# LoRA products of a gated FFN as six-row products in four row groups of TensorE, with another PSUM layout and another place for the fold transpositions

## The chip, the cores and the metric

The kernel runs on one NeuronCore of a Trainium2 chip (trn2). Its metric is the device time in microseconds, as a median over runs. Five engines work side by side: PE (TensorE, matrix products), DVE (VectorE), ACT (ScalarE), POOL (GpSimd) and SP (SyncE, which here only issues transfers). PE reads from SBUF and writes to PSUM, which has eight banks of 512 fp32 values for each of 128 partitions.

## The reference

One post-norm transformer block over 2 x 1024 tokens of width 1024, in fp32. The first half is a gated unit of hidden width 2752 in which, for each token, the half of the silu values of the smallest magnitude is set to zero. The second half is a gated FFN with quantised-style weights (a quarter of the input width, repeated four times) and LoRA terms of rank 2. Cut to what matters here:

```python
def _qlora_linear(x, wq, A, B):
    w = jnp.tile(wq, (1, 4))
    base = x @ w.T
    lora = x @ A.T @ B.T
    return base + lora * 0.5

def _L0_ffn_ref(x, w1q, a1, b1, w3q, a3, b3, w2q, a2, b2):   # h = 2752, d = 1024, rank 2
    gate = silu(_qlora_linear(x, w1q, a1, b1))
    up = _qlora_linear(x, w3q, a3, b3)
    return _qlora_linear(gate * up, w2q, a2, b2)

x = layernorm(x + attn(x, w_gate, w_up, w_down))
x = layernorm(x + ffn(x, w1q, a1, b1, w3q, a3, b3, w2q, a2, b2))
```

## The kernel before

The 2048 tokens are 16 tiles of 128, in four groups of four tiles (`GT = 4`). The program runs through three parts: `gate_up` (products with w_gate and w_up, and the search for the median magnitudes), `down` (products with w_down, then the first layernorm), and the FFN. Every fp32 product is made of products of a rounded high part and a low part (fp32r): high by high, high by low, low by high. `split` makes the two parts, the high one on ACT (L173), the low one on POOL or DVE (L174).

The FFN works group by group (`ffn`). It has two halves:

- **f1**, the first products. Since the weights repeat four times along the input, the token's 1024 values are first added up to 256 ("fold", on POOL, L927 to L929), so that a product has two chunks of 128. The hidden width 2752 is cut into eight column blocks of 344 (`NB`, `BW`). An item is one tile and one block: `f1_mm` makes gate and up products in two PSUM banks (a pair), ACT takes silu of the first (L987), DVE multiplies it by the second (L988) and by the two rows of a2 (L990), ACT sums those (L992), POOL adds the results of blocks that share second weights into hf (L994). The order is block by block, and in a block tile by tile.
- **f2**, the second products. hf is transposed (L1026), split into hh and hl (L1028, L1029), and multiplied by w2 in `run_ops` (L765); cm holds the last 48 columns and the LoRA sums. Then come the residual sum (L768) and the layernorm.

The LoRA term of f1 is x A^T B^T. The four numbers x A^T of each token (two for gate, two for up) are in `dall`. `f1_tile` writes them into a tile tl, for each of gate and up six columns: high part, high part again, low part. `f1_tile2` transposes the two fold chunks (L949) and two shifted views of tl (L951), so that each of gate and up has its six rows at the top of its own 128-row matrix in fh; ACT copies (L954), DVE makes the low part fl (L955). The tile br holds, in rows 0 to 5 and 32 to 37, the B weights of gate and up in the matching order (high, low, high), with zeros elsewhere. A LoRA product is then one ordinary product of 128 rows, last in its bank (L984):

```python
for c in range(2):
    nc.tensor.matmul(o, fh[:, c, :], wh[:, c, :], start=c == 0, stop=False)      # L981
    nc.tensor.matmul(o, fh[:, c, :], wl[:, c, :], start=False, stop=False)       # L982
    nc.tensor.matmul(o, fl[:, c, :], wh[:, c, :], start=False, stop=False)       # L983
nc.tensor.matmul(o, fh[:, 2 + w, :], self.br[:, bs], start=False, stop=True)     # L984
```

So an item has 14 products of 128 x 128 by 128 x 344, and two of them are LoRA products: 16 tiles x 8 blocks x 2 = 256 in all.

br is built during the last `down` group by `ffn_consts`: SP loads the raw rows (L810), ACT and POOL split them, and two small copies on ACT's own transfer queue (L813) put the low part in place. The four tiles of the first group are prepared in that time too (`f1_first`); those of the following groups while the group before them is in f1.

What sets the order: `item` keeps two queues. It calls an item's loads at once, its preparation up to two items later and its products up to two more items later (`q1`, `q2`), so that loads are issued ahead and `down` runs into the FFN without a stop; `flush` empties both queues. A scheduler then orders the recorded instructions for each engine; on the chip each engine runs its own list in order, and waits on semaphores for the others. PSUM from `down` on is one pool, psb: three pairs of banks, tag mm, for products, and two single banks, tag tp, for transpositions. A buffer is handed on in rotation, when its last reader is done.

Of the kernel before, what the change touches and what calls it, by code (L numbers as in the profile page):

```python
# [7 lines left out]
F = mybir.dt.float32  # L8
# [10 lines left out]
P = 128  # L19
# [46 lines left out]
class Kern:  # L66
# [8 lines left out]
    def run(self):  # L75
# [3 lines left out]
        with ExitStack() as es:  # L79
# [38 lines left out]
            self.gate_up()  # L118
            self.lasta = self.lastv = self.lastd = None
            ps_es.close()  # L120
            psb = es.enter_context(tc.tile_pool(name="psb", bufs=1, space=PSUM, reuse_waits="tile"))
            self.pair = lambda: psb.tile([P, 2, 512], F, tag="mm", bufs=3, name="mm")
            self.tpb = lambda: psb.tile([P, 4, P], F, tag="tp", bufs=2, name="tp")
            x_es.close()
# [18 lines left out]
            self.fcg = self.ffn_consts()  # L143
            list(self.down(ng - 1, f1=2))
            self.dp_es, self.fp2 = dp_es, None
            for g in range(ng):
                self.ffn(g)
            self.flush()
# [640 lines left out]
    def ffn_consts(self):  # L789
        nc, fp = self.nc, self.fp  # L790
        A = self.A
        self.br = fp.tile([P, NI], R, name="br")
        self.abc = fp.tile([P, 4, H], F, name="abc")
        self.fst, self.c2 = {}, False
        for i in range(4):
            yield
            with self.load_behind():
                nc.sync.dma_start(
                    self.abc[:, i, :], A[("a1", "a3")[i // 2]][i % 2 : i % 2 + 1, :].partition_broadcast(P)
                )  # L800
        for b in range(NB):
            yield
            bs = slice(b * BW, (b + 1) * BW)
            sv = fp.tile([P, 2, BW], F, tag="sv", bufs=2, name="braw")
            raw, lo = sv[:, 0], sv[:, 1].bitcast(R)
            nc.gpsimd.memset(raw, 0.0)
            with self.load_behind():
                for w, n in ((0, "b1t"), (32, "b3t")):
                    for i in range(3):
                        nc.sync.dma_start(raw[w + 2 * i : w + 2 * i + 2, :], A[n][:, bs])  # L810
            self.split(self.br[:, bs], lo, raw)
            for w in (0, 32):
                nc.scalar.dma_start(self.br[w + 2 : w + 4, bs].bitcast(F), lo[w + 2 : w + 4, :].bitcast(F))  # L813

    def dots_down(self):
        xt, a1, a3 = (self.tk.tile([P, NI], F, tag=f"a{i}", name=n) for i, n in ((0, "dx"), (1, "da"), (3, "db")))
# [37 lines left out]
    def ffn(self, g):  # L854
        tiles = [t for t in range(g * GT, (g + 1) * GT) if t < self.nt]
        for b in range(NB):
            ws = []
            if tiles[-1] + 1 < self.nt:
                if b % 2 == 0:
                    if b:  # L860
                        self.f1_tile2(tiles[-1] + b // 2)
                    self.f1_tile(tiles[-1] + 1 + b // 2)
            for t in tiles:
                self.item(
                    lambda: self.f1_prep(b, ws),
                    lambda: None,
                    lambda st=self.fst[t], b=b, ws=ws: self.f1_mm(st, b, ws),
                    2, 2,
                )
        if tiles[-1] + 1 < self.nt:  # L870
            self.f1_tile2(tiles[-1] + GT)
        ws = []
        for t in tiles:
            self.item(
                lambda: self.f2_w(ws),
                lambda t=t: self.f2_prep(self.fst[t], t),
                lambda st=self.fst[t], t=t, ws=ws: self.f2_mm(st, t, ws),
                2, 1,
            )

# [34 lines left out]
    def f1_tile(self, t, f=None):  # L915
# [13 lines left out]
        G.tensor_tensor(f, f, x2[:, 768:1024], ALU.add)  # L929
        dr = sm.tile([P, 4], R, tag="dr", name="dr")  # L930
        V.tensor_copy(dr, d)
        tl = fp.tile([P, P + 6], F, tag="tl", bufs=1, name="tl")
        G.memset(tl, 0.0)
        d2 = d.rearrange("p (w r) -> p w r", w=2)
        dr2 = dr.bitcast(F).rearrange("p (w r) -> p w r", w=2)
        for w in range(2):
            q = 38 * w
            V.tensor_copy(tl[:, q : q + 2], dr2[:, w])
            V.tensor_copy(tl[:, q + 2 : q + 4], dr2[:, w])
            V.tensor_tensor(tl[:, q + 4 : q + 6], d2[:, w], dr2[:, w], ALU.subtract)  # L940
        st["f"] = f, tl

    def f1_tile2(self, t):
# [3 lines left out]
        tp = self.tpb()  # L947
        for c in range(2):
            nc.tensor.transpose(tp[:, c, :], f[:, c * P : (c + 1) * P], self.ident)  # L949
        for w in range(2):  # L950
            nc.tensor.transpose(tp[:, 2 + w, :], tl[:, 6 * w : 6 * w + P], self.ident)  # L951
        fh = fp.tile([P, 4, P], R, tag="fh", bufs=6, name="fh")
        fl = fp.tile([P, 2, P], R, tag="fl", bufs=6, name="fl")
        nc.scalar.copy(fh, tp)  # L954
        V.tensor_tensor(fl, tp[:, 0:2, :], fh[:, 0:2, :].bitcast(F), ALU.subtract)  # L955
        st["f"] = fh, fl

    def f1_mm(self, st, b, ws):
        nc, fp = self.nc, self.fp
        V, G = nc.vector, nc.gpsimd  # L960
        bs = slice(b * BW, (b + 1) * BW)
# [10 lines left out]
            st["hf"] = self.fp2.tile([P, 688], F, tag="hf", bufs=5, name="hf")  # L972
            st["part"] = self.sm.tile([P, 2, NB], F, tag="part", bufs=6, name="part")
        hf, part = st["hf"], st["part"]
        pp = self.pair()
        ps = [pp[:, w, :BW] for w in range(2)]
        for w in range(2):
            o = ps[w]
            wh, wl = ws[w]
            for c in range(2):  # L980
                nc.tensor.matmul(o, fh[:, c, :], wh[:, c, :], start=c == 0, stop=False)  # L981
                nc.tensor.matmul(o, fh[:, c, :], wl[:, c, :], start=False, stop=False)  # L982
                nc.tensor.matmul(o, fl[:, c, :], wh[:, c, :], start=False, stop=False)  # L983
            nc.tensor.matmul(o, fh[:, 2 + w, :], self.br[:, bs], start=False, stop=True)  # L984
        hs = slice((b % 2) * BW, (b % 2 + 1) * BW)
        gt = hf[:, hs] if b < 2 else self.fp2.tile([P, BW], F, tag="gt", bufs=3, name="gt")
        nc.scalar.activation(gt, ps[0], AF.Silu)  # L987
# [104 lines left out]
```

## Time and profile before

| | us |
|---|---|
| median of 3 runs | 1923.64 |
| lowest and highest | 1919.69, 1924.59 |
| the profiled execution, its own time | 1926.91 |
| its span, first to last instruction | 1925.1 |
| first f1 product in it | 1466.5 |

The profile is of one execution; its granted TensorE clock was 0.993 of full speed. Its page gives busy times and shares of the span for each engine, groups of instructions by line with their mean duration, and what ended the idle time ahead of them. L984 is line 984 of the kernel above. A product's recorded duration contains the time in which it drains, and the next one may start before it ends; so durations of PE rows can't be added up, and start-to-start distances are used instead. PEld rows are the weight loads, one for each product. ACTq, SPq and the like are instructions of an engine's sequencer, such as the issue of a transfer. In the table by stage the cuts are where f1 begins and ends in each group.

### The profile page before, as it was taken

How to read it: one execution, taken by the hardware profiler on the slowest of the kernel's cores; microseconds unless marked ns; L12 is line 12 of the kernel's file. 1: busy time of each engine (PE TensorE's matmuls, PEld its weight loads, DVE VectorE, ACT ScalarE, POOL GpSimd, SP SyncE). 2: the span in 40 equal slices, each digit the busy share in tenths (PEclk: the TensorE clock that was granted, in tenths of full speed). 3: DMA queues.
4: the chain of work that ended last, by engine and by line, in shares of the span. 5: the costliest groups of instructions: out<-in, count | busy, mean ns of one | idle time of the engine just before them, and what ended most of it. 6: DMA issues, size and time to landing. Idle time of an engine off the chain costs nothing. (4 is left out here: it accounts for less than half of the span.)

```text
span 1925.1 us, 29381 instructions
## 1 busy us (share of the span) xinstructions
PE 1885.3 (98%) x10825; PEld 1754.4 (91%) x10825; DVE 1229.6 (64%) x1831; ACT 904.0 (47%) x1448; POOL 973.0 (51%) x606
## 2 busy tenths in 40 slices
PE   9999999999999999999999999999998999998998
PEld 9999999999999999999888787888787979898896
DVE  4633556767358574691238998688467857779565
ACT  4333477414883258622246533323333746557362
POOL 5655664445445354355565443554565746436062
PEclk9999999999999999999999999999999999999999
DMA  7677687676977868667798756977776878485651
GB/s 266 237 250 260 236 325 261 210 272 253 330 231 241 314 235 303 236 228 256 282 328 285 270 188 227 337 245 261 268 250 244 279 284 321 155 318 177 229 196 66
DMA packets 166205, 488.66 MB, mean 254 GB/s; under 512 B 24772, under 2 KB 45380, under 8 KB 166056
## 3 DMA queue, kind: packets, MB, share of 16 engines
q1 hardware_dynamic: 165848, 486.43, 71.9%
q8 instruction: 85, 1.39, 0.3%
q14 instruction: 64, 0.52, 0.1%
q10 hardware_dynamic: 208, 0.31, 0.0%
HBM read 370.30 MB, written 116.33 MB: 253 GB/s over the span
## 5 line engine op out<-in xcount | busy, mean ns | idle before, releaser
L174 POOL TENSOR_TENSOR wl<-wr,wh 128x1376 fp32r<-128x1376 f32 (+2 forms) x187 | 566.4, 3035 | 466.1 <-ACT wh L173 436.8
L353 PE MATMUL mm<-wh,xh 128*128 128x344 f32 x1928 | 610.4, 322 | 2.8 <-DMA wh<-tw3T1h 2.8
L353 PE MATMUL mm<-wh,xl 128*128 128x344 f32 x1928 | 609.8, 320 | 0.0
L173 ACT CAST wh<-wr 128x1376 fp32r<-128x1376 f32 (+2 forms) x192 | 232.4, 1215 | 340.9 <-PE mm L353 199.6
L353 PEld LDWEIGHTS mm<-wh,xh 128*128 128x128 f32 x1928 | 364.7, 189 | 3.0 <-issue 3.0
L353 PEld LDWEIGHTS mm<-wh,xl 128*128 128x128 f32 x1928 | 364.6, 189 | 0.0
L353 PE MATMUL mm<-wl,xh 128*128 128x344 f32 x1928 | 342.1, 319 | 0.0
L353 PEld LDWEIGHTS mm<-wl,xh 128*128 128x128 f32 x1928 | 310.1, 188 | 0.0
L765 PE MATMUL mm<-wh,mh 128*128 128x512 f32 x680 | 217.8, 400 | 0.1
L765 PE MATMUL mm<-wl,mh 128*128 128x512 f32 x680 | 215.1, 395 | 1.1 <-POOL wl L174 1.1
L765 PE MATMUL mm<-wh,ml 128*128 128x512 f32 x648 | 205.5, 396 | 0.8 <-DVE ml L750 0.8
L460 ACT ACTIVATE jk<-a,cur 128x2752 int8<-128x2752 f32 x66 | 170.8, 2588 | 31.2 <-DVE cur L482 15.8
L994 POOL TENSOR_TENSOR hf<-hf,gt 128x344 f32<-128x344 f32 x96 | 142.2, 1491 | 75.6 <-DVE gt L988 68.7
L725 POOL TENSOR_TENSOR m<-m,ub 128x512 f32<-128x512 f32 (+2 forms) x93 | 111.0, 1194 | 128.0 <-ACT ub L724 65.8
L981 PE MATMUL mm<-wh,fh 128*128 128x344 f32 x512 | 166.2, 325 | 5.8 <-DVE gt L988 5.2
L983 PE MATMUL mm<-wh,fl 128*128 128x344 f32 x512 | 164.0, 320 | 0.0
L982 PE MATMUL mm<-wl,fh 128*128 128x344 f32 x512 | 163.9, 320 | 0.0
L765 PEld LDWEIGHTS mm<-wl,mh 128*128 128x128 f32 x680 | 127.4, 188 | 30.1 <-POOL wl L174 2.2
L768 DVE TENSOR_TENSOR acc<-acc,mm 128x1024 f32<-128x1024 f32 x96 | 116.4, 1214 | 57.9 <-PE mm L765 27.8
L765 PEld LDWEIGHTS mm<-wh,mh 128*128 128x128 f32 x680 | 124.7, 189 | 24.8 <-ACT mh L749 0.5
L765 PEld LDWEIGHTS mm<-wh,ml 128*128 128x128 f32 x648 | 121.2, 189 | 26.9 <-DVE ml L750 1.0
L992 ACT ACTIVATE pa<-pa 128x344 f32<-128x344 f32 x256 | 123.0, 483 | 38.6 <-DVE pa L990 34.0
(191 smaller groups left out, 2742.5 us busy)
## 6 DMA issues: line engine op xcount, KB each, us to landing
wr<-wu SPq DMA_DIRECT2D x64, 688.0 KB
wr<-wg SPq DMA_DIRECT2D x52, 688.0 KB
wr<-wd SPq DMA_DIRECT2D x48, 512.0 KB
s_d<-cc SPq DMA_DIRECT2D x64, 344.0 KB
m_d<-mt SPq DMA_DIRECT2D x64, 344.0 KB
a<-s_d SPq DMA_DIRECT2D x64, 344.0 KB
wl<-wc_w SPq DMA_DIRECT2D x48, 344.0 KB
wh<-wc_w SPq DMA_DIRECT2D x48, 344.0 KB
```

What stands on the lines that cost most here:

```text
L173: self.lasta = self.nc.scalar.copy(hi, raw)
L174: (eng or self.nc.gpsimd).tensor_tensor(lo, raw, hi.bitcast(F), ALU.subtract)
L353: self.nc.tensor.matmul(o, l, r, start=start and n < m and n % (2 * KH) == 0, stop=stop and n >= m and (n - m) % KH == KH - 1)
L460: nc.scalar.activation(jk.bitcast(I8), av[j], AF.Sign, bias=t, scale=-1.0, accum_out=s)
L725: nc.gpsimd.tensor_tensor(m[:, :w], m[:, :w], ub[:, :w], ALU.mult)
L765: nc.tensor.matmul(ps[:, h], a, b[:, h * 512 : (h + 1) * 512], start=i == 0, stop=i == len(ops) - 1)
L768: nc.vector.tensor_tensor(out, out, ps.rearrange("p a b -> p (a b)"), ALU.add)
L981: nc.tensor.matmul(o, fh[:, c, :], wh[:, c, :], start=c == 0, stop=False)
L982: nc.tensor.matmul(o, fh[:, c, :], wl[:, c, :], start=False, stop=False)
L983: nc.tensor.matmul(o, fl[:, c, :], wh[:, c, :], start=False, stop=False)
L992: nc.scalar.activation(pa[:, r], pa[:, r], AF.Copy, scale=0.5, accum_out=part[:, r, b : b + 1])
L994: G.tensor_tensor(hf[:, hs], hf[:, hs], gt, ALU.add)
```

## The change

- **LoRA products.** tl gets 128 columns. The six columns of gate and up stand at 0 and 32 for even tiles and at 64 and 96 for odd tiles; one transposition instead of two brings them to the same rows of fh, which now has three chunks. br's rows 0 to 63 are copied to rows 64 to 127, by one more transfer for each block on ACT's queue. For every second tile, `f1_mm` takes two PSUM pairs at once and opens all four banks with four products of six rows each, at rows 0, 32, 64 and 96, which are four row groups of the array; they stand first in their banks. The 12 other products of each tile follow.
- **PSUM.** After the last `down` group both queues are flushed and psb is closed. A new pool psc gives the FFN four pairs; a transposition takes a pair too, and uses its first bank.
- **Fold transpositions.** `f1_tile` and `f1_tile2` for the next group's tiles were called while an item's loads were recorded. Now they are called with the item's products, two to four items later, ahead of the first product of the block.

```diff
@@ run
-            psb = es.enter_context(tc.tile_pool(name="psb", bufs=1, space=PSUM, reuse_waits="tile"))
+            psb_es = ExitStack()
+            psb = psb_es.enter_context(tc.tile_pool(name="psb", bufs=1, space=PSUM, reuse_waits="tile"))
...
             self.dp_es, self.fp2 = dp_es, None
+            self.flush()
+            psb_es.close()
+            psc = es.enter_context(tc.tile_pool(name="psc", bufs=1, space=PSUM, reuse_waits="tile"))
+            self.pair = lambda: psc.tile([P, 2, 512], F, tag="mm", bufs=4, name="mm")
+            self.tpb = lambda: self.pair()[:, 0].rearrange("p (a b) -> p a b", a=4)
@@ ffn_consts
+            nc.scalar.dma_start(self.br[64:P, bs].bitcast(F), self.br[0:64, bs].bitcast(F))
@@ ffn
-            if tiles[-1] + 1 < self.nt:
-                if b % 2 == 0:
-                    if b:
-                        self.f1_tile2(tiles[-1] + b // 2)
-                    self.f1_tile(tiles[-1] + 1 + b // 2)
+            pre = []
+            if tiles[-1] + 1 < self.nt and b % 2 == 0:
+                if b:
+                    pre.append(lambda b=b: self.f1_tile2(tiles[-1] + b // 2))
+                pre.append(lambda b=b: self.f1_tile(tiles[-1] + 1 + b // 2))
...
-                    lambda st=self.fst[t], b=b, ws=ws: self.f1_mm(st, b, ws),
+                    lambda st=self.fst[t], t=t, b=b, ws=ws, pre=pre: ([pre.pop(0)() for _ in pre[:]], self.f1_mm(st, t, b, ws)),
@@ f1_tile
-        tl = fp.tile([P, P + 6], F, tag="tl", bufs=1, name="tl")
+        tl = fp.tile([P, P], F, tag="tl", bufs=1, name="tl")
...
-            q = 38 * w
+            q = 32 * w + t % 2 * 64
@@ f1_tile2
-        for w in range(2):
-            nc.tensor.transpose(tp[:, 2 + w, :], tl[:, 6 * w : 6 * w + P], self.ident)
-        fh = fp.tile([P, 4, P], R, tag="fh", bufs=6, name="fh")
+        nc.tensor.transpose(tp[:, 2, :], tl, self.ident)
+        fh = fp.tile([P, 3, P], R, tag="fh", bufs=6, name="fh")
...
-        nc.scalar.copy(fh, tp)
+        nc.scalar.copy(fh, tp[:, 0:3])
@@ f1_mm
-        pp = self.pair()
-        ps = [pp[:, w, :BW] for w in range(2)]
+        if t % 2 == 0:
+            self.pp = [self.pair() for _ in range(2)]
+            for j in range(2):
+                for w in range(2):
+                    q = slice(64 * j + 32 * w, 64 * j + 32 * w + 6)
+                    nc.tensor.matmul(
+                        self.pp[j][:, w, :BW], self.fst[t + j]["f"][0][q, 2, :], self.br[q, bs], start=True, stop=False
+                    )
+        ps = [self.pp[t % 2][:, w, :BW] for w in range(2)]
...
-                nc.tensor.matmul(o, fh[:, c, :], wh[:, c, :], start=c == 0, stop=False)
+                nc.tensor.matmul(o, fh[:, c, :], wh[:, c, :], start=False, stop=False)
                 nc.tensor.matmul(o, fh[:, c, :], wl[:, c, :], start=False, stop=False)
-                nc.tensor.matmul(o, fl[:, c, :], wh[:, c, :], start=False, stop=False)
-            nc.tensor.matmul(o, fh[:, 2 + w, :], self.br[:, bs], start=False, stop=True)
+                nc.tensor.matmul(o, fl[:, c, :], wh[:, c, :], start=False, stop=c == 1)
```

More of the change, by code (lines that the diff above doesn't have):

```diff
@@ L866, in ffn @@
                     lambda: None,
-                    lambda st=self.fst[t], b=b, ws=ws: self.f1_mm(st, b, ws),
+                    lambda st=self.fst[t], t=t, b=b, ws=ws, pre=pre: ([pre.pop(0)() for _ in pre[:]], self.f1_mm(st, t, b, ws)),
                     2, 2,
                 )
-        if tiles[-1] + 1 < self.nt:
-            self.f1_tile2(tiles[-1] + GT)
+        pre = [lambda: self.f1_tile2(tiles[-1] + GT)] if tiles[-1] + 1 < self.nt else []
         ws = []
@@ L876, in ffn @@
                 lambda t=t: self.f2_prep(self.fst[t], t),
-                lambda st=self.fst[t], t=t, ws=ws: self.f2_mm(st, t, ws),
+                lambda st=self.fst[t], t=t, ws=ws, pre=pre: ([pre.pop(0)() for _ in pre[:]], self.f2_mm(st, t, ws)),
                 2, 1,
@@ L949, in f1_tile2, with f1_mm @@
             nc.tensor.transpose(tp[:, c, :], f[:, c * P : (c + 1) * P], self.ident)
-        for w in range(2):
-            nc.tensor.transpose(tp[:, 2 + w, :], tl[:, 6 * w : 6 * w + P], self.ident)
-        fh = fp.tile([P, 4, P], R, tag="fh", bufs=6, name="fh")
+        nc.tensor.transpose(tp[:, 2, :], tl, self.ident)
+        fh = fp.tile([P, 3, P], R, tag="fh", bufs=6, name="fh")
         fl = fp.tile([P, 2, P], R, tag="fl", bufs=6, name="fl")
-        nc.scalar.copy(fh, tp)
+        nc.scalar.copy(fh, tp[:, 0:3])
         V.tensor_tensor(fl, tp[:, 0:2, :], fh[:, 0:2, :].bitcast(F), ALU.subtract)
         st["f"] = fh, fl
-    def f1_mm(self, st, b, ws):
+    def f1_mm(self, st, t, b, ws):
         nc, fp = self.nc, self.fp
```

## The prediction

> **What bounds the kernel now.** I read the page's totals and its 40 slices first, then the table by stage, then the PE rows in order of time inside two stages, and the list of waits last.
>
> ```profile
> span 1925.1 us, 29381 instructions
> ...
> PE 1885.3 (98%) x10825; PEld 1754.4 (91%) x10825; DVE 1229.6 (64%) x1831; ACT 904.0 (47%) x1448; POOL 973.0 (51%) x606
> ```
>
> Of these, only PE is near the span. The change touches the FFN, the last 460 us, so the stages there count. In the table by stage below, the columns are PE, PEld, DVE, ACT and POOL busy (instructions), granted clock, DMA share and GB/s. The four rows are the four first-FFN stages (f1), one for each group of four token tiles.
>
> ```profile
> 1466.50:1551.40 84.90, 80.30 (x483) 76.76 (x482) 70.33 (x117) 56.96 (x168) 60.64 (x49) 0.98 0.81 278
> ...
> 1589.20:1662.40 73.20, 73.20 (x470) 72.92 (x469) 53.63 (x104) 47.44 (x157) 47.64 (x43) 1.00 0.77 277
> ...
> 1696.90:1775.10 78.20, 74.57 (x471) 72.95 (x470) 72.01 (x109) 59.08 (x179) 42.73 (x37) 1.00 0.73 245
> ...
> 1810.60:1882.40 71.80, 71.80 (x458) 71.59 (x457) 46.87 (x76) 45.55 (x155) 37.51 (x26) 1.00 0.66 229
> ```
>
> In the second and fourth stages PE never rests; every other engine has 20 us or more to spare. In the third, DVE is busy 72.0 of 78.2 us, and PE waits for it. The PE rows in order of time give the price of one product (start, duration):
>
> ```profile
> 1818.86 0.32 PE L983 MATMUL mm<-wh,fl 128*128 128x344 f32 x1
> 1819.02 0.32 PE L984 MATMUL mm<-br,fh 128*128 128x344 f32 x1
> 1819.17 0.32 PE L981 MATMUL mm<-wh,fh 128*128 128x344 f32 x1
> ```
>
> Starts lie 0.157 us apart although a product takes 0.32 us: a product costs 0.157 as long as the next may enter while it drains. L984 is the LoRA product, at the full price although only 6 of its 128 rows carry data. What a product costs when nothing may overlap shows where PE had run dry:
>
> ```profile
> 1754.52 0.32 PE L984 MATMUL mm<-br,fh 128*128 128x344 f32 x1
> 1755.41 0.42 PE L981 MATMUL mm<-wh,fh 128*128 128x344 f32 x1 [0.57 <-DVE gt L988]
> 1755.67 0.32 PE L982 MATMUL mm<-wl,fh 128*128 128x344 f32 x1
> ```
>
> The first product after the gap is 0.42 long and the second starts 0.26 behind it: 0.105 us more than in the stream, for a weight load that nothing covered. So draining costs 0.32 - 0.157 = 0.163 and restarting 0.105.
>
> **The change part by part.** The order in which the changed program's instructions stand tells what the scheduler made of it, and I work from that.
>
> *Removed:* 256 products L984: 256 x 0.157 = -40.2 us. One of two transpositions of tl per tile: 16 at the 0.11 us by which transpositions follow each other: -1.8.
>
> *Added products:* 256 six-row products. In the source four stand together, for two tiles. In the compiled order only 21 fours are left; 86 groups are pairs, since the second tile's two products were put later, behind their wait for a free PSUM pair. That is 107 groups instead of 64. If the members of a group run beside each other, a group costs one product: 107 x 0.157 = +16.8. No row of this trace has less than 128 rows, so it can't say whether they do. The nearest row, the transpositions' 0.11 us for each 128-column weight load, would add 149 further members x 0.11 = +16.4. The Trainium skill (TensorE: Matmul & The Clock Gate, Part 3: Packing small matmuls) has products in different row groups start about 4 ns apart, +0.6. The transpositions all use the same rows and are not near in just that, so I take the page's and keep +16.4 for the range.
>
> *Added switches of the array:* each group goes from 128-row to 32-row products and back, 214 switches. This is where a rule speaks against the change. The trace shows only one form, 128 by 128, always overlapped. The Trainium skill (TensorEngine Tiling (Array Packing), Key Properties) says that changing the tiling mode, unlike changing the tile, drains the engine. By the rows alone, without the rule, the switches are free and the sum is -30 us. With it, each switch lets the product in flight run out (0.163), and the next weight load is uncovered (0.105, the restart above): 0.268 x 214 = +57.4. The bounds for one switch are 0 and 0.352 (0.163 plus a whole recorded weight load of 0.189). I take 0.268, the trace's own price for running dry and restarting.
>
> *Fold transpositions later:* at the opening of the first stage, PE's order has three tiles' transpositions at its head, with f1 work behind them:
>
> ```profile
> 1478.78 0.41 PE L951 MATMUL tp<-ident,tl 128*128 128x128 f32 x2 [0.38 <-DVE tl L940]
> 1481.06 0.44 PE L949 MATMUL tp<-ident,fold 128*128 128x128 f32 x2 [1.87 <-POOL fold L929]
> 1481.34 0.38 PE L951 MATMUL tp<-ident,tl 128*128 128x128 f32 x2
> 1482.23 0.42 PE L981 MATMUL mm<-wh,fh 128*128 128x344 f32 x1 [0.51 <-DVE hf L988]
> ```
>
> Four gaps between 1477.5 and 1482.2 hold 3.6 us beyond the work, and the clock then stands at 0.50 from 1483.2 to 1486.6, worth 1.7. In the new order these transpositions stand eight items (a tile and a column block each) apart. Bounds -5.3 and 0; I take -4. In the new order the first h transpositions of the closing FFN half (f2) also stand two items before the end of f1; before, PE waited there for ACT's copy hh, with gaps of 3.0, 0.9 and 1.0 us in stages one to three. I take -3 of 4.9. POOL's memset of tl becomes 128 columns (3.4 us in all before), and ACT's fh copy three quarters as long (9.3 us in all, under PE): nothing, covered by 10 us or more of POOL and ACT idle time per stage.
>
> *Four PSUM pairs, two taken at a time:* the third stage's five waits PE mm L981 <- DVE gt L988 (4.8 us of gaps between its PE rows) are PE being ahead of DVE. With 29 groups costing PE 29 x (0.157 + 0.536) = 20.1 us in place of 64 x 0.157 = 10.0, PE falls behind DVE, and these waits go: -4. Against it, a transposition now takes one of the four pairs, so a pair returns one tile earlier than before. What stands behind such a wait on PE is the rest of the stage; the scheduler moved the second tile's products behind up to 11 others to cover it. Some 12 times, 0.25 us, bounds 0 and 1 each: +3.
>
> *Flush, br and the queues:* flush finishes the down products before the FFN loads; SP's first w1 load now stands behind four 512 KB weight loads and the last masks. Eight new 88 KB copies of br stand on ACT's queue. Each waits until two earlier copies have landed, and with it ACT and everything behind, above all mh, which PE needs. How that looks is in the trace:
>
> ```profile
> 1366.88 5.28 ACTq L813 DMA_DIRECT2D br<-braw  x3
> 1372.26 0.59 ACT L749 CAST mh<-tp 128x512 fp32r<-128x512 f32 x1 [6.39 <-DMA br<-braw]
> ```
>
> A stop of 6.4 us; PE, with three items queued, lost 1.8 us soon after it. Eight more issues at 0.57 us and their waits lie mostly under that cover. If it is gone each costs PE one or two us. Together +3, bounds -1 and +12.
>
> *Sum:* -40.2 - 1.8 - 4 - 3 - 4 + 16.8 + 57.4 + 3 + 3 = +27.2 us. The profiled execution took 1926.91 (span 1925.1), so 1954; against the median of 1923.64 that is 1951.
>
> **The rivals.** *The switch is free and the groups overlap* (faster). The sum without 57.4 is -30.2. But then DVE stays ahead in time in the third stage: PE needs 384 x 0.157 + 29 x 0.157 + 1.3 = 66 us, DVE 72, so that stage ends at 74 at the earliest, not at 68; +5.7. That gives -24.5: 1899. For it: rows with gaps show PE restarting at once, and the weight loads run ahead of products in flight. Against: the rule. The deciding point is one switch at 0.141 us ((57.4 - 27.2) / 214): below it the kernel is faster, above it slower.
>
> *Only the tail is paid,* 0.163 a switch, weights loaded meanwhile: -22.5 on my sum, 1928. For it: weight loads lie 0.157 ahead of their products everywhere in the stream. Against: a load for another mode may itself have to wait.
>
> *Dear switches and paced groups:* 0.352 a switch (+18) and members 0.11 apart (+16.4): 1985. For it: the weight loads' busy share, 91%, leaves this lane little room.
>
> *It doesn't do what it says* holds in part already: 86 of 107 groups are pairs. Were all 64 fours kept, 43 x 0.693 = 30 us less would be paid and my sum would be about -3; so the split is what makes the likeliest case slow.
>
> **How the numbers follow.** A measurement of this kernel can tell about 0.3% (6 us) from no change. My case 0.38 (1940 to 1965), tail only 0.20 (1918 to 1940), dear 0.20 (1965 to 2000), free 0.22 (1890 to 1912). Faster: the free case and a fringe of the tail case, 0.25. Same: the middle of the tail case, 0.07. Slower: 0.68. The range cuts half of the free case and half of the dear one: 1898 to 1983.
>
> **What would show it.** In the stream of f1, the gap from the last 128-row start to a group's first start, and from its last start to the next 128-row start: 0.43 each in my case (0.157 + 0.268), 0.32 for the tail, 0.16 if free. Between members: near zero, or 0.11. Stages two and four: with 27 and 23 groups at 0.693 in place of 64 products at 0.157 each, 73.2 and 71.8 us should become some 81 and 78; in the free case 67 and 65. The opening of the first stage should show no gap over 1 us. If PE has gaps of over 1 us before the groups with DVE as releaser, the pair waits were underestimated; if the down stage before 1466 grows by more than 5 us, br's copies were.

## The result, and the profile after

The changed kernel takes 1942.43 us (median of 6 runs, 1940.50 to 1948.87) against 1921.51 for the kernel before (6 runs): +20.9 us, ratio 1.0111 with a 95% interval of 1.0096 to 1.0125. It is slower, inside the range, 9 us below the predicted 1951. The sum behind that number is right only in total: two of its terms are wrong, in opposite directions.

The profiled execution took 1943.85 us. The page's totals:

```profile
span 1942.1 us, 29330 instructions
...
PE 1903.1 (98%) x10809; PEld 1734.8 (89%) x10809; DVE 1243.3 (64%) x1831; ACT 903.1 (46%) x1448; POOL 977.4 (50%) x606
```

PE's busy time grew by 17.8 us and the span by 17.0. The table by stage, with the columns as before (length, then PE, PEld, DVE, ACT, POOL busy, granted clock, DMA share, GB/s):

```profile
1467.90:1556.40 88.50, 81.74 (x464) 70.45 (x464) 75.64 (x108) 59.18 (x175) 62.22 (x48) 0.94 0.80 277
1592.80:1670.00 77.20, 76.85 (x463) 66.63 (x463) 57.12 (x107) 47.46 (x158) 44.41 (x39) 1.00 0.75 265
1705.90:1790.10 84.20, 80.76 (x463) 68.86 (x463) 74.23 (x113) 59.01 (x181) 48.05 (x38) 0.96 0.65 224
1825.70:1900.10 74.40, 73.67 (x455) 64.99 (x455) 50.25 (x77) 44.87 (x154) 36.10 (x26) 1.00 0.62 223
```

Stages two and four, where PE had no rest before, went from 73.2 and 71.8 us to 77.2 and 74.4. I had said 81 and 78, or 67 and 65 with free switches: it is between. Stages one and three also lost clock, 0.94 and 0.96 for 0.98 and 1.00.

The rows of PE in order of time (start, duration) show a group of four among full products:

```profile
1829.80 0.32 PE L995 MATMUL mm<-wh,fl 128*128 128x344 f32 x1
1830.05 0.43 PE L985 MATMUL mm<-br,fh 6*128 6x344 f32 x4
1830.41 0.42 PE L993 MATMUL mm<-wh,fh 128*128 128x344 f32 x1
1830.67 0.31 PE L994 MATMUL mm<-wl,fh 128*128 128x344 f32 x1
1830.83 0.32 PE L995 MATMUL mm<-wh,fl 128*128 128x344 f32 x1
```

L985 is the six-row product, L993 to L995 are the full ones. As medians over the whole trace: 0.250 from the last full start to the group's first start, 0.003 from one member to the next, 0.350 from the last member to the next full start, 0.262 from that to the second one, 0.157 from there on. Four six-row products run as one, as I had taken them to. A group costs 0.250 + 0.350 + 0.262 - 2 x 0.157 = 0.55 us, 0.549 with the unrounded medians (pairs add one 0.003 and fours three). Of that 0.157 is the product itself, so the two switches cost 0.392. The weight loads of the same stretch (PEld) show what the price is made of:

```profile
1829.64 0.19 PEld L995 LDWEIGHTS mm<-wh,fl 128*128 128x128 f32 x1
1830.05 0.19 PEld L985 LDWEIGHTS mm<-br,fh 6*128 6x128 f32 x4 [0.22 <-issue]
1830.41 0.19 PEld L993 LDWEIGHTS mm<-wh,fh 128*128 128x128 f32 x1 [0.17 <-issue]
1830.52 0.19 PEld L994 LDWEIGHTS mm<-wl,fh 128*128 128x128 f32 x1
```

In the stream a load starts 0.154 us ahead of its own product, beside the product in flight: L995 at 1829.64 for the product at 1829.80. At a switch it does not. The loads of the group, and later that of the first full product, start together with their own product (0.002 ahead in the median), and that product's row is 0.42 long instead of 0.32. So each switch, in either direction, costs a wait until the load may start and then a load that nothing covers. Going in, the wait is 0.250 - 0.157 = 0.093; its uncovered load, 0.105, lies inside the group's row. Coming out, the wait is 0.350 - 0.105 - 0.157 = 0.088; its load shows as 0.262 instead of 0.157 ahead of the second full product. That is some 0.2 us for each switch, where I had 0.268: 0.163 of wait and 0.105 of load.

The opening of the first stage, with its 3.6 us of gaps before, is now one dense stream; transpositions stand between items, and PE waits for none of them:

```profile
1485.98 0.32 PE L995 MATMUL mm<-wh,fl 128*128 128x344 f32 x1
1486.14 0.38 PE L955 MATMUL mm<-ident,fold 128*128 128x128 f32 x2
1486.36 0.27 PE L956 MATMUL mm<-ident,tl 128*128 128x128 f32 x1
1486.56 0.42 PE L985 MATMUL mm<-br,fh 6*128 6x344 f32 x2
```

But the same stage has a larger gap 48 us later (the bracket holds PE's idle time and its releaser):

```profile
1534.19 0.32 PE L995 MATMUL mm<-wh,fl 128*128 128x344 f32 x1
1539.39 0.65 PE L985 MATMUL mm<-br,fh 6*128 6x344 f32 x2 [4.88 <-DVE gt L999]
1539.97 0.66 PE L993 MATMUL mm<-wh,fh 128*128 128x344 f32 x1
```

The group waits for a free PSUM pair, and that pair for DVE's product gt (L999). DVE's and POOL's rows of the same stretch say why gt was late:

```profile
1534.17 1.58 DVE L180 TENSOR_TENSOR wl<-wr,wh 128x688 fp32r<-128x688 f32 x1
1535.67 2.30 DVE L946 TENSOR_TENSOR tl<-dall,dr 128x2 f32<-128x2 f32 x1
...
1538.83 0.93 DVE L999 TENSOR_TENSOR gt<-gt,mm 128x344 f32<-128x344 f32 x2
```

```profile
1534.98 2.97 POOL L180 TENSOR_TENSOR wl<-wr,wh 128x1024 fp32r<-128x1024 f32 x1
```

A weight split and the next tile's tl stand ahead of gt in DVE's list. L946 subtracts two columns, 0.15 us as a rule, and here takes 2.30: it ends with POOL's split, at 1537.97 and 1537.95. It is not the whole of the gap: ACT's two silus for gt (L998) ran from 1535.70 to 1536.48, so by an estimate from these rows the first pair could have been free near 1536.6, and about 2 of the 4.9 us would have remained. The third stage has a gap of its own, where the h transpositions (L1037), now inside f1, wait for POOL; the row by stretch below it gives the granted clock, the value after the POOL column:

```profile
1779.13 0.44 PE L1037 MATMUL mm<-ident,hf 128*128 128x128 f32 x2
1782.27 0.90 PE L1037 MATMUL mm<-ident,hf 128*128 128x128 f32 x3 [2.71 <-POOL hf L1005]
```

```profile
1783.10:1788.00 4.90, 4.90 (x17) 3.94 (x16) 2.42 (x8) 2.93 (x11) 1.90 (x2) 0.50 0.11 35
1539.40:1549.60 10.20, 10.20 (x34) 8.57 (x35) 8.43 (x11) 6.66 (x22) 5.93 (x5) 0.51 0.96 347
```

Behind each of the two gaps PE runs at half clock, for 6.8 and 10.2 us.

On ACT's queue the new copies (L820) stand where I had them; the stop of 6.4 us is as long as before, and the first f1 product comes at 1467.9 instead of 1466.5:

```profile
1364.96 5.01 ACTq L819 DMA_DIRECT2D br<-braw  x3
1370.07 0.59 ACT L755 CAST mh<-tp 128x512 fp32r<-128x512 f32 x1 [6.40 <-DMA br<-braw]
...
1373.96 1.18 ACTq L820 DMA_DIRECT2D br<-br  x2
```

**An account of the four f1 stages.** I compared each start-to-start distance on PE with the usual one of its kind (0.157 between full products, the distances above at groups, 0.11 and 0.246 at transpositions). What is left over is put down to waits, or to half clock (a granted clock of 0.5) where the clock was low; the usual distances are medians, and a wait can end inside a stretch at half clock, so these two columns are good to some 2 us. "Six-row" is from the last full start ahead of a group to the first one behind it. In us, summed over the four stages; the last four rows belong to the experiments:

| kernel | length | full products | six-row | transpositions | waits | half clock |
|---|---|---|---|---|---|---|
| before | 308.0 | 285.4 | 0 | 8.7 | 12.3 | 1.5 |
| after | 323.6 | 237.1 | 63.6 | 3.7 | 12.2 | 6.9 |
| full rows | 314.1 | 280.7 | 0 | 7.9 | 21.4 | 4.1 |
| fours | 319.7 | 239.8 | 39.2 | 3.7 | 24.0 | 13.1 |
| own pair | 328.7 | 236.6 | 75.6 | 3.7 | 9.8 | 3.0 |
| groups apart | 427.9 | 270.1 | 153.4 | 4.0 | 0.5 | 0 |

Against before: products +15.3 (some +19 without 18 products of `down`, which stood inside the first stage, from 1466.82 to 1470.95, and now stand ahead of it; by the rows -40.2 + 107 x 0.549 = +18.5 were to come), transpositions -5.0, waits -0.1, half clock +5.4, together +15.6. The f2 halves add 1.3, so the FFN, from the first f1 product to PE's last product, went from 449.7 to 466.6; with the 4.1 us of `down` products that left this stretch, the same work takes 21.0 us more, as much as the medians' +20.9.

### The profile page after: what moved, and what is told of

It reads as the page before. It is cut to its first block, busy times and chain, and to the rows that moved or that the text cites. A ratio compares the mean times of both kernels' runs of the same rounds, so it can differ in the third digit from the quotient of the medians.

```text
span 1942.1 us, 29330 instructions
## 1 busy us (share of the span) xinstructions
PE 1903.1 (98%) x10809; PEld 1734.8 (89%) x10809; DVE 1243.3 (64%) x1831; ACT 903.1 (46%) x1448; POOL 977.4 (50%) x606
## 5 line engine op out<-in xcount | busy, mean ns | idle before, releaser
L1005 POOL TENSOR_TENSOR hf<-hf,gt 128x344 f32<-128x344 f32 x96 | 144.2, 1516 | 78.5 <-DVE gt L999 77.2
L993 PE MATMUL mm<-wh,fh 128*128 128x344 f32 x512 | 174.6, 341 | 0.0
L995 PE MATMUL mm<-wh,fl 128*128 128x344 f32 x512 | 166.1, 325 | 0.0
L1003 ACT ACTIVATE pa<-pa 128x344 f32<-128x344 f32 x256 | 123.0, 483 | 40.2 <-DVE pa L1001 37.9
```

The costliest lines, as they stand in the source:

```text
L993: nc.tensor.matmul(o, fh[:, c, :], wh[:, c, :], start=False, stop=False)
L1003: nc.scalar.activation(pa[:, r], pa[:, r], AF.Copy, scale=0.5, accum_out=part[:, r, b : b + 1])
L1005: G.tensor_tensor(hf[:, hs], hf[:, hs], gt, ALU.add)
```

## The experiments

In all runs below "FFN" is that stretch in the run's profiled execution. Ahead of it executions differ by several us even where nothing was changed: f1 starts at 1466.5 in the profile of the kernel before, at 1462.1 in a second profile of the same kernel, and at 1460.1 with only a buffer moved. So the FFN stretch is the better measure of place, and the median that of size. In all versions but the kernel before, fold later alone and the last two of the table, 18 products of `down` (4.1 us) stand ahead of f1 instead of inside its first stage; for the same work their FFN is 4.1 us longer than the table says.

| run | median, us | ratio (95%) | FFN, us |
|---|---|---|---|
| before | 1921.4 to 1923.0 | 1 | 449.7 |
| after | 1942.43 | 1.0111 (1.0096 to 1.0125) | 466.6 |
| full rows | 1935.03 | 1.0062 (1.0048 to 1.0076) | 457.2 |
| fours | 1939.99 | 1.0095 (1.0081 to 1.0110) | 462.8 |
| own pair | 1950.70 | 1.0156 (1.0142 to 1.0171) | 471.8 |
| fold later alone | 1927.32 | 1.0030 (1.0015 to 1.0045) | 453.1 |
| fold early | 1945.48 | 1.0118 (1.0097 to 1.0140) | 465.5 |
| fours, fold early | 1941.13 | 1.0099 (1.0079 to 1.0120) | 460.5 |
| four pairs alone | 1927.71 | 1.0031 (1.0019 to 1.0043) | 452.8 |
| br copies alone | 1929.37 | 1.0036 (1.0021 to 1.0050) | 453.2 |
| groups apart | 2047.70 | 1.0649 (1.0632 to 1.0666) | 568.9 |
| groups twice | 2011.54 | 1.0466 (1.0447 to 1.0485) | 529.1 |
| before again | 1923.45 | 1.0001 (0.9991 to 1.0010) | 450.3 |
| buffer moved | 1922.17 | 0.9995 (0.9985 to 1.0005) | 449.3 |

### The price of a switch

**Own pair.** From the changed kernel; each tile opens its own pair, so that the order holds 127 groups of almost only two instead of 107.

```diff
-        if t % 2 == 0:
-            self.pp = [self.pair() for _ in range(2)]
...
+        pp = self.pair()
+        for w in range(2):
+            q = slice(t % 2 * 64 + 32 * w, t % 2 * 64 + 32 * w + 6)
+            nc.tensor.matmul(pp[:, w, :BW], fh[q, 2, :], self.br[q, bs], start=True, stop=False)
```

> The changed kernel, but each tile takes one PSUM pair and opens it with its own two six-row products, at its own two row groups; the order has 127 groups (2 of four, 123 of two, 2 single ones) in place of 107. Switch theory: 20 x 0.549 = 11 us more, about 1953 us. Pair-wait rival: a pair is taken one tile later and gets free earlier, so PE waits less: 1935 us or less.

Measured 1950.70, 8 us over the changed kernel for 20 more groups, where 20 x 0.549 = 11 were to come. The cleanest place is the fourth stage, in which PE never waits:

```profile
1828.20:1906.90 78.70, 78.51 (x454) 66.26 (x454) 47.68 (x77) 44.65 (x154) 37.39 (x26) 1.00 0.60 207
```

32 groups and 78.7 us against 23 groups and 74.4: 0.48 per group (0.58 if the gap of 0.9 us that the changed kernel has there is taken out). So the number of groups sets the time: in the account six-row products take 12.0 us more. The pair-wait rival is right that PE waits less (waits and half clock fall by 6.3), but that is the smaller part.

**Groups apart and groups twice.** From the own-pair kernel. In the first each tile and block has its two six-row products twice, with two full products between; in the second the passes stand together, behind the two full products. The diff is that of groups apart; groups twice moves its last three lines ahead of the loop over k.

```diff
+        for k in range(2):
             for w in range(2):
                 q = slice(t % 2 * 64 + 32 * w, t % 2 * 64 + 32 * w + 6)
-                nc.tensor.matmul(pp[:, w, :BW], fh[q, 2, :], self.br[q, bs], start=True, stop=False)
+                nc.tensor.matmul(pp[:, w, :BW], fh[q, 2, :], self.br[q, bs], start=True, stop=k == 0)
+            for w in range(2):
+                if k == 0:
+                    nc.tensor.matmul(pp[:, w, :BW], fh[:, 0, :], ws[w][0][:, 0, :], start=True, stop=True)
```

> Each tile takes one pair of its own (as in the run where every tile has its own two six-row products), and for each tile and column block the two six-row products come twice, with two full products between the two passes; the first pass and the two full products are overwritten. This adds 128 groups and 256 full products. Revised theory (a group costs 0.549 us, as the rows of the changed kernel give it): 1951 + 128 x (0.549 + 2 x 0.157) = 2061 us. With the 0.693 of my prediction: 2080. If the loss of the own-pair kernel were waits and not switches (a group worth one product, 0.157): 2011.

> The same instructions as in the kernel with the groups apart, but both passes of the six-row products stand directly behind each other, so there are 128 groups of four instead of 256 of two. The second pass uses the same rows as the first and so should take its turn, 0.157 us: 1951 + 128 x (2 x 0.157 + 0.157) = 2011 us. The difference to the kernel with the groups apart is 128 pairs of switches and nothing else: 128 x 0.392 = 50 us by the rows of the changed kernel, 128 x 0.536 = 69 by my prediction, 0 if switches are free.

Measured 2047.7 and 2011.5; groups twice met its number, groups apart missed by 13. The rows of PE, groups apart first, then groups twice:

```profile
1661.31 0.31 PE L995 MATMUL mm<-wh,fl 128*128 128x344 f32 x1
1661.55 0.42 PE L984 MATMUL mm<-br,fh 6*128 6x344 f32 x2
1661.91 0.57 PE L987 MATMUL mm<-wh,fh 128*128 128x344 f32 x2
1662.41 0.43 PE L984 MATMUL mm<-br,fh 6*128 6x344 f32 x2
1662.77 0.42 PE L993 MATMUL mm<-wh,fh 128*128 128x344 f32 x1
1663.03 0.32 PE L994 MATMUL mm<-wl,fh 128*128 128x344 f32 x1
```

```profile
1659.62 0.48 PE L982 MATMUL mm<-wh,fh 128*128 128x344 f32 x2
1660.03 0.58 PE L986 MATMUL mm<-br,fh 6*128 6x344 f32 x4
1660.54 0.43 PE L992 MATMUL mm<-wh,fh 128*128 128x344 f32 x1
1660.81 0.31 PE L993 MATMUL mm<-wl,fh 128*128 128x344 f32 x1
```

From 1661.31 to 1663.03 are 1.72 us, in which four full products take 0.63: 0.55 for each of two groups. In the other kernel a start lies 0.16 behind 1659.62 (two products in one row), and from there to 1660.81 are 1.03 us; less two full products that is 0.72, one group and one more pass of 0.16. So a second pass through the same rows costs one product and no switch. This kernel also shows the two parts of a switch apart (medians of its 128 groups): the second pass starts 0.258 behind the first, 0.157 and the uncovered load of the first pass; from the second pass, whose loads were covered, to the next full start are 0.245 instead of 0.350, 0.157 and the wait of 0.088 alone. In the second and fourth stages, where PE is the only bound in both, the table gives 106.9 and 105.9 us against 94.8 and 93.7; the row of the second stage of each, groups apart first:

```profile
1611.80:1718.70 106.90, 106.90 (x592) 82.80 (x592) 54.73 (x98) 47.38 (x157) 43.64 (x38) 1.00 0.55 188
```

```profile
1606.60:1701.40 94.80, 94.80 (x591) 80.89 (x590) 54.81 (x98) 45.64 (x157) 43.04 (x38) 1.00 0.61 209
```

12.1 and 12.2 us for 32 pairs of switches, 0.38 each, against 0.392 by the rows. The medians differ by 36 and not by 50: in stages one and three the slower kernel loses its waits (its account has 0.5 us), so part of the added work lies where PE had waited. That is also why groups apart stayed 13 us under the 2061 counted from own pair, which has 12.8 us of waits and half clock. The switch has a price, and it is some 0.2 us, not free, and not 0.268.

### Pairs or fours

**Fours.** From the changed kernel; the first full product of each chunk is held behind the last six-row product, which keeps 62 fours and 4 twos.

```diff
-                    nc.tensor.matmul(
+                    self.lora = nc.tensor.matmul(
...
-                nc.tensor.matmul(o, fh[:, c, :], wh[:, c, :], start=False, stop=False)
+                with self.tc.issue_after(self.lora.ins):
+                    nc.tensor.matmul(o, fh[:, c, :], wh[:, c, :], start=False, stop=False)
```

> The changed kernel, with a tile's 12 products held behind the last LoRA product of its group, so that the compiled order has 62 groups of four and 4 of two (66 groups in place of 107). Switch theory: 41 x 0.549 = 22.5 us less, less what PE then waits for the second pair of banks: 1920 to 1930 us. Pair-wait rival (waits for a free PSUM pair are the cost): PE now waits for two pairs before each group with nothing to do meanwhile, so slower than the changed kernel, over 1945 us.

Measured 1939.99: neither. Stages two and four gained 3 us each over the changed kernel, and the fourth is below the 71.8 us of the kernel before:

```profile
1597.20:1671.50 74.30, 71.85 (x464) 65.17 (x464) 56.07 (x105) 47.48 (x158) 43.10 (x39) 1.00 0.76 273
...
1827.60:1898.60 71.00, 69.76 (x454) 63.63 (x454) 49.88 (x77) 44.83 (x154) 35.17 (x26) 1.00 0.66 230
```

That is what the price of a group says: a four costs 0.549 and the four full products that it replaces 0.628. But in stages one and three waits and half clock take it back (37.1 us together in the account of the four stages, 19.1 in the changed kernel). **Fours with the fold early** was to remove these waits: the order of the kernel before for fold and h transpositions, and all 64 fours held.

```diff
-                    lambda st=self.fst[t], t=t, b=b, ws=ws, pre=pre: ([pre.pop(0)() for _ in pre[:]], self.f1_mm(st, t, b, ws)),
+                    lambda st=self.fst[t], t=t, b=b, ws=ws: self.f1_mm(st, t, b, ws),
...
+                with self.tc.issue_after(self.lora.ins):
+                    nc.tensor.matmul(o, fh[:, c, :], wh[:, c, :], start=False, stop=False)
```

> As the kernel with early transpositions, and every four is held together (64 fours, no pairs). By the rows of the changed kernel a group costs 0.549 us, so 64 x 0.549 = 35.1 us stand in place of 40.2: -5. The rest of the change without later transpositions costs 13.6 - 6 = 7.6 by the first runs. Theory (switches, and the early order leaves PSUM pairs free in time): 1921 - 5 + 8 = 1924, up to 1930 with waits for the second pair. Rival (the wait for two free pairs, not the order of the fold, made the gaps of the kernel with held fours): still gaps of 2 to 3 us with DVE as releaser in stages one and three, half clock behind them, and 1936 to 1940.

Measured 1941.13, far above the theory's number and 1 us above the rival's range; the rival's reason holds. PE's rows show a four that comes apart at its wait for the second pair:

```profile
1525.27 0.32 PE L997 MATMUL mm<-wh,fl 128*128 128x344 f32 x1
1525.52 0.42 PE L986 MATMUL mm<-br,fh 6*128 6x344 f32 x2
1528.14 0.42 PE L986 MATMUL mm<-br,fh 6*128 6x344 f32 x2 [2.20 <-DVE gt L1001]
```

So the gain of fours, at most 64 x 0.079 = 5 us, needs two free pairs at one moment, and DVE doesn't return them in time.

### The rest of the change

**Full rows.** From the changed kernel; all is kept but the LoRA products, which have 128 rows again (and tl its two transpositions).

```diff
-                    q = slice(64 * j + 32 * w, 64 * j + 32 * w + 6)
                     nc.tensor.matmul(
-                        self.pp[j][:, w, :BW], self.fst[t + j]["f"][0][q, 2, :], self.br[q, bs], start=True, stop=False
+                        self.pp[j][:, w, :BW], self.fst[t + j]["f"][0][:, 2 + w, :], self.br[:, bs], start=True, stop=False
```

> All of the change is kept (four PSUM pairs, two taken at a time, flush, br copies, later fold transpositions, the same split into 21 fours and 86 pairs); only the LoRA products are ordinary 128-row products again, with the old tl and its second transposition. Switch theory (the trace of the changed kernel: a group of six-row products costs 0.252 + 0.349 + 0.262 - 2 x 0.157 = 0.549 us on PE, 107 groups 58.7 us): 256 products at 0.157 (40.2 us) and 16 transpositions (1.8) instead of 58.7, so 17 us below the changed kernel, about 1926 us. Rival (the pool of four pairs, the flush and the br copies made it slower, and six-row products are as cheap as meant): no gain, 1940 us or more, since 149 more products are paid.

Measured 1935.03, between the two. The six-row products account for 7.4 of the 20.9 us, and 13.6 are there without them, where my sum had a gain. In the list of waits of its first three stages, PE waits for pairs (L985 <- gt) and for hf:

```profile
PE mm L985 <- DVE gt L999: 11.7, 8, 5.1
PE mm L1037 <- POOL hf L1005: 5.5, 3, 3.0
```

The account says why 20.0 us of added product time (63.6 + 237.1 - 280.7) become 9.4 of FFN: it holds 21.4 us of waits with full rows and 12.2 with six, and 4.2 us less of transpositions, against 2.8 more of half clock. The likely reason is that PE, busier, meets its buffers later and waits less.

**Fold later alone.** The kernel before with only the later calls of `f1_tile` and `f1_tile2`.

```diff
-                        self.f1_tile2(tiles[-1] + b // 2)
-                    self.f1_tile(tiles[-1] + 1 + b // 2)
+                    pre.append(lambda b=b: self.f1_tile2(tiles[-1] + b // 2))
+                pre.append(lambda b=b: self.f1_tile(tiles[-1] + 1 + b // 2))
```

> The kernel before with one part of the change alone: the fold and its transpositions for the next group are called with the products. The prediction gave this part -4 us (the four gaps at the opening of the first stage, 3.6 us, and the half clock behind them, 1.7 us), and -3 us for the h transpositions that stand earlier; if both come from this part, 1915 us. Rival: the gaps only move to another place in the first stage (POOL's fold is late anyway), so no difference to before within 2 us.

Measured 1927.32, 5.9 us slower; my -4 and -3 both fail. At the opening of the first stage a gap of 3.04 us stays, ahead of the first full product behind the transpositions. The third stage waits for DVE seven times (five before), and the stage grew by 2 us; the f2 halves grew by 0.8 to 1.3 us each in the first three groups:

```profile
PE mm L980 <- DVE gt L987: 4.9, 7, 1.0
```

**Fold early.** The reverse: the changed kernel with the calls where they were before.

```diff
-                    pre.append(lambda b=b: self.f1_tile2(tiles[-1] + b // 2))
-                pre.append(lambda b=b: self.f1_tile(tiles[-1] + 1 + b // 2))
+                        self.f1_tile2(tiles[-1] + b // 2)
+                    self.f1_tile(tiles[-1] + 1 + b // 2)
```

> The changed kernel with one part undone: the fold and h transpositions are issued where the kernel before issues them; six-row products, four PSUM pairs, flush and br copies stay (88 pairs and 20 fours in the order, 108 groups). By the first runs, later transpositions alone cost the kernel before about 6 us. If they cost the same inside the change: 1942 - 6 = 1936 us, and the stop of 5 us in the first stage and of 2.9 us at the end of the third are gone from PE's rows. Rival, they are a gain inside the change (as my sum had it, 4 + 3 us) because a transposition now takes one of the four pairs: 1945 or more.

Measured 1945.48, which goes to the rival, though the two ratios (1.0118 and 1.0111) can't be told apart. The stop at the end of a stage is not gone but larger, now in the first, as its list of waits says:

```profile
PE mm L1038 <- POOL hf L1006: 5.4, 1, 5.4
```

So the place of the fold is not an addend: it costs 6 us in the kernel before and nothing that can be told in the changed one, where the h transpositions wait for POOL inside f1 in both orders.

**Four pairs alone.** The kernel before with `flush`, the four pairs, and transpositions that take a pair.

```diff
+            self.flush()
+            psb_es.close()
+            psc = es.enter_context(tc.tile_pool(name="psc", bufs=1, space=PSUM, reuse_waits="tile"))
+            self.pair = lambda: psc.tile([P, 2, 512], F, tag="mm", bufs=4, name="mm")
+            self.tpb = lambda: self.pair()[:, 0].rearrange("p (a b) -> p a b", a=4)
```

> The kernel before with the PSUM part alone: flush ahead of the FFN, four pairs instead of three pairs and two transposition banks, a transposition takes a pair; LoRA products, fold and br copies as before. Theory (of the 13.6 us that the change costs without row groups, some 6 come from later transpositions, the rest from taking two pairs at once with the LoRA products first): 1921 to 1925. Rival (the flush and the lost transposition banks carry the rest): 1927 to 1931, with the start of f1 2 to 4 us later than 1466.5 and gaps at transpositions.

Measured 1927.71, in the rival's range. The rival's later f1 can't be read from one profile: f1 starts at 1464.1, between the 1466.5 and 1462.1 of the kernel before. Its gaps at transpositions are there. The list of waits over the first three stages has, beside the waits for pairs, stops of the h transpositions (L1032) inside f1; in the kernel before these stand at the start of f2:

```profile
PE mm L987 <- DVE gt L994: 7.3, 8, 1.4
PE mm L1032 <- POOL hf L1000: 4.3, 3, 1.6
PE mm L1032 <- DVE fl L961: 3.4, 1, 3.4
```

**br copies alone.** The kernel before with the one new line of `ffn_consts`.

```diff
+            nc.scalar.dma_start(self.br[64:P, bs].bitcast(F), self.br[0:64, bs].bitcast(F))
```

> The kernel before with the eight new copies of br on ACT's queue alone (rows 64 and up get the same values; the LoRA products of 128 rows meet zeros there, so nothing else moves). Theory (covered, as I had it, a few us at most): 1920 to 1924, f1 starts within 1 us of 1466.5. Rival (each new copy stops ACT about 1 us beyond PE's cover): 1925 to 1931, f1 starts 3 or more us later.

Measured 1929.37: the size is the rival's, 6.4 us, the place is not. f1 starts at 1466.4, which does not show that `down` grew: the two profiles of the kernel before have 1466.5 and 1462.1, with 4.1 us less ahead of it. The first stage grew from 84.9 to 87.9 although those 4.1 us left it, and the other three are within 0.2 us of what they were:

```profile
1466.40:1554.30 87.90, 79.19 (x469) 76.47 (x469) 70.20 (x117) 58.07 (x171) 61.94 (x50) 0.94 0.78 268
```

The eight transfers also change the scheduler's order (the last 18 `down` products stand ahead of f1), and the first stage has 4.8 us of waits for gt (1.6 before) and a clock of 0.94 (0.98 before). Which of the two, the copies or the order, brings the loss was not separated.

**Before again, and a buffer moved.** Three parts that cost 5 to 6 us each made me ask what nothing costs. The first is the kernel before itself; the second widens tl by 100 columns and leaves every instruction where it is.

```diff
-        tl = fp.tile([P, P + 6], F, tag="tl", bufs=1, name="tl")
-        G.memset(tl, 0.0)
+        tl = fp.tile([P, P + 6 + 100], F, tag="tl", bufs=1, name="tl")
+        G.memset(tl[:, : P + 6], 0.0)
```

> The kernel before, unchanged: what a comparison of this kind shows where nothing differs, and a second profile of it. Ratio 1.000 within 0.0015. If the parts run alone (4 to 6 us each) are within what repetition gives, this shows a like difference.

> The kernel before with tl's buffer 100 columns wider, so that what lies behind it in its pool moves by 400 bytes; every engine's instructions stay as they are and where they are. If the 4 to 6 us that each part of the change costs alone are its own work: 1921 to 1925 here. If any disturbance of this program costs that much: 1926 to 1929.

Ratios 1.0001 and 0.9995, FFN 450.3 and 449.3. So the parts' 5 to 6 us are real, and the FFN stretch repeats within 1 us. There fold later shows 3.4 us, four pairs and br copies 3.1 and 3.5, which with the 4.1 us of `down` products that left the stretch are 7.2 and 7.6, no less than their medians (4.8 and 6.4): these two losses lie in the FFN. For fold later 2.5 us lie outside it or in executions that were not profiled; that stays open. Alone the three parts add up to 17.1 us, together, in full rows, the change costs 13.6: they are not addends.

## Why the prediction was right, and which steps were wrong

- **Six-row members overlap: right.** 0.003 us from one to the next. What I took from the Trainium skill (TensorE: Matmul & The Clock Gate, Part 3: Packing small matmuls), about 4 ns, holds here, and the alternative of 0.11 is excluded.
- **Switches: the mechanism was right, the size of one of its two terms was not.** +57.4 was the largest term. By the rows it is 107 x 0.392 = +41.9, so removed and added products, tl and switches come to +16.7 where I had +32.2 (without the transpositions +18.5). I let each switch wait until the product in flight had run out, 0.163, and then load weights uncovered, 0.105. PEld's rows show these two things at every switch, in both directions, and the load is as long as I said. The term that was mis-sized is the wait: 0.09 instead of 0.163, so the load starts some 0.07 ahead of the recorded end of the product in flight, and 214 times that is the 15 us. What the Trainium skill says (TensorEngine Tiling (Array Packing), Key Properties), that changing the mode drains the engine, shows as a price here, but that price is not a product's whole recorded tail. The tail-only rival, 0.163 with the weights loaded meanwhile, has the mechanism the wrong way round: the tail is shorter, and the weights are not loaded meanwhile. The sum of the two, some 0.2, lies above the 0.141 at which I put the turn. My sign of 0.43 for both distances was off even in my own case: a product's row starts with its load, so the load going in does not show in the distance to the group's first start.
- **Groups: right.** 107 in the compiled order, 86 of them pairs, and they make the loss of the products themselves: a pair costs 0.549 for 0.314 saved, a four 0.549 for 0.628. But that the split is what makes the kernel slow was wrong: with nearly all or all fours kept it is still some 18 us slower than the kernel before. That keeping all fours would save 30 us was too much: at the measured price it is 43 x 0.549 = 24, and they saved 2.4, since they bring waits of their own.
- **Opening of the first stage, -4: wrong as a gain, and in its cause.** Its gaps are gone, as said, and no gap there is over 1 us. But the later fold calls are not what removed them: alone they leave a gap of 3.04 us there, while four pairs alone and fold early, with the calls where they were, have none over 1 us. And waits of the four stages are 12.2 us, about as before (12.3), and half clock rose by 5.4: the wait turned up 48 us later, behind a weight split and tl's columns on DVE.
- **h transpositions earlier, -3: wrong.** PE no longer waits at f2's start but two items ahead of it, for POOL's hf (2.7 us in the third stage), and the f2 halves together are 1.3 us longer.
- **Waits of the third stage, -4: half right.** PE does fall behind DVE there, and its waits for gt all but go. The gap of 2.9 us for hf and the half clock behind it (2.6 us in that stage) take their place.
- **Pair waits +3, flush, br and the queues +3: too low for the parts alone.** Four pairs with flush cost 4.8 us and the br copies 6.4. Whether `down` grew can't be told closely: f1 starts 1.4 us later than in one profile of the kernel before and 5.8 later than in the other, and 4.1 us of products were moved ahead of it.
- **The sum.** With measured sizes: +16.7 for products, switches and tl instead of +32.2; waits and half clock +5.3 instead of the net -8 of the three credits and the pair waits; transpositions -5.0 instead of -1.8. So the switch term was 15.5 too dear and the waits 13 too cheap: 27.2 - 15.5 + 13.3 - 3.2 = 21.8. That the total of +27.2 came near +20.9 is owed to these two errors having opposite signs. "Faster" would have needed a switch below some 0.1 us; with the waits as forecast alone, the kernel would still be some 8 us slower.
- **A better version** did not come out: each of the three parts run alone is slower than the kernel before, six-row products were not run in the old PSUM layout, and the one place with a gain, fours in the fourth stage, gains 0.8 us against it.

## What to carry to other kernels

Packing small products into row groups pays by the group, not by the product: here a group costs 0.55 us inside a stream of full products, so it must replace at least four of 0.157 each, and it must still be that large in the compiled order. Look up how many of the intended groups the scheduler kept before pricing them. A wait that an edit removes is a gain only if the next producer on the same path is early; when a buffer's owner is a loaded engine (here DVE for pairs, POOL for hf), the gap comes back elsewhere, and a gap of 2 to 5 us can also cost half clock afterwards.

## What the runs showed of the hardware

- A switch between 128-row and six-row products costs the same two things in both directions: a wait of 0.09 us (0.093 in, 0.088 out) until the next weight load starts, and that load uncovered, 0.105 us. In a stream of one kind the load starts 0.154 us ahead of its product; at a switch it starts with it. A second pass over the same row groups, right behind the first (groups twice), costs one product more and no second switch.
- A tiny DVE instruction can cost as much as POOL's big one beside it: L946, two columns, 2.30 us instead of 0.15, ending with POOL's split of 2.97 us; in the same stage a copy of two columns (L944) took 1.62 us beside a POOL split of 1.67 and ended 0.03 us behind it. The Trainium skill (SBUF — State Buffer, SBUF: two separate sides) says that DVE and GpSimd share a pair of ports as an exclusive lock, also for a DVE instruction with two SBUF inputs beside a GpSimd one that reads SBUF, as L946 and the split are, and that the later one is blocked for the whole instruction; the rows fit that. No run moved the split away, so that it is the cause was not tried.
- Gaps of 2.9 and 5.0 us were followed by half clock for 6.8 and 10.2 us. No length of a single gap decides it here: in the groups-twice kernel a gap of 3.15 us in the third stage was followed by none (clock 1.00 throughout the stage), and one of 2.1 us in the first by 10.2 us at 0.50.
